# Two load stretches in the middle instead of one, larger output slots, and stores held behind the loads

## The chip, the cores and the metric

The kernel runs on one core of one Trainium2 chip. The metric is the device time of one execution in microseconds (us), the median of three runs. The profiled execution is a further run with its own time.

## The reference

For each of 4096 rows the input `x` has 32 fields of 64 numbers. Every field is multiplied by one 64x64 matrix `W`, and for every pair of fields i < j the output is the elementwise product of field i with the transformed field j:

```python
vid = jnp.einsum('bfd,de->bfe', x, W)
idx_i, idx_j = jnp.triu_indices(32, k=1)
return x[:, idx_i, :] * vid[:, idx_j, :]     # (4096, 496, 64), float32
```

There are 496 pairs, so 33.6 MB are read and 520.1 MB written.

## The kernel before

**Tiles and units.** The host lays the input out so that a partition holds one of 2 x 64 embedding positions and the free dimension holds 128 rows. A *unit* is one field, or one product, of 128 rows: 128 partitions x 128 float32, 512 bytes in a partition and 65,536 bytes in all. A tile is 32 units of input and gives 496 units of output. There are 16 tiles, so 7936 units go out. On-chip memory is one tensor `mem` of 445 units; inputs and finished products share it. The matrix product `vid` of the current tile (32 units) fills all of PSUM.

**Order of the work.** TensorE computes `vid` of a tile in two halves, fields 16 to 31 (high) and then 0 to 15 (low), 8 matmuls each. VectorE (DVE) multiplies pairs, first those among the high fields (120 units), then the 16x16 block of low x high (256 units), then those among the low fields (120 units). When the last product that reads a half of `vid` is done, VectorE raises `free` and TensorE may fill that half for the next tile; it raises `there` when it is full. `by_block` lists the blocks, and `products` cuts them into VectorE instructions where a slot or a seam in it ends (`BREAKS`).

**Slots.** `SLOTS` is a table made ahead by hand or by a planner: entry (size, home, seams...) says that the next `size` units of output are put into `mem` from unit `home` on, and stored with one DMA when they are complete. A seam is a place inside the slot at which an instruction must end, so that the part behind it can wait for something of its own. An instruction that writes units waits until every earlier store that reads those units has landed (`after`).

**Loads.** `GROUPS` says at which tile a group of inputs begins and in which pieces (lowest and highest unit of `mem`) it is loaded. Before, tile 0 comes with two small loads, tiles 1 to 7 with three pieces right behind (224 units), and tiles 8 to 15 with three pieces (256 units) whose DMAs stand in the program at the start of tile 8. A load waits until the units it overwrites have been read and stored.

**The queue.** Every DMA, load or store, is issued by SyncE (SP) in the order of the program (`transfer`, L169). So whatever SP waits for, everything later waits as well. The first store after a group of loads waits for the landing of the last piece but one (`hold[-2]`, L272). `Queue.waits` leaves out waits that an earlier one implies.

Of the kernel before, what the change touches and what calls it, by code (L numbers as in the profile page):

```python
# [10 lines left out]
P = 128  # L11

C = 128
# [1 line left out]
UNITS = 445  # L15


TOP = 256


GROUPS = [
    (0, [(96, 224), (26, 96), (0, 26)]),
    (8, [(154, 256), (26, 154), (0, 26)]),
]


SLOTS = [
# [10 lines left out]
]  # L38


# [4 lines left out]
STARTS = [0, *accumulate(n for n, *_ in SLOTS)]  # L45


BREAKS = sorted({a + s for a, (_, _, *seams) in zip(STARTS, SLOTS) for s in seams} | set(STARTS))


def by_block():


    def within(lo):
        yield "step", lo, 2, 1, 0
        for k in range(2):
            yield "step", lo, 4, 2, k
        for i in (lo, lo + 8):
            yield "row", i + 4, i, 4, 4
        yield "row", lo + 8, lo, 8, 8  # L60

    yield from within(16)
    yield "row", 16, 0, 16, 16
    yield from within(0)


def products(blocks, at=0):

    for kind, a, b, c, d in blocks:
        if kind == "row":  # L70
            rows, n, i0, di, j0, dj = c, d, b, 0, a, 1
        else:
            rows, n, i0, di, j0, dj = 16 // b, c, a, b, a + c + d, b
        r = k = 0
        while r < rows:
            room = BREAKS[bisect_right(BREAKS, at)] - at
            if k or room < n:
                m, w = 1, min(n - k, room)
            else:
                m, w = min(rows - r, room // n), n  # L80
            yield at, m, w, i0 + r * di + k, di, j0 + r * dj, dj
            at += m * w
            if k + w == n:
                r, k = r + m, 0
            else:
                k += w


def pairs(blocks):

    for _, m, w, i, di, j, dj in products(blocks):
        for r in range(m):
            for k in range(w):
                yield i + r * di + k, j + r * dj


class Queue:
# [33 lines left out]
def place_of(t, fields):  # L131

    first = max(begin for begin, _ in GROUPS if begin <= t)
    return TOP - (t - first + 1) * fields


def ends(tiles):
    return [begin for begin, _ in GROUPS[1:]] + [tiles]
# [6 lines left out]
def pairwise_bilinear_kernel(nc, x0, x, out):  # L145
# [5 lines left out]
    HALF = F // 2  # L151

    ctx = ExitStack()
    mem = ctx.enter_context(nc.sbuf_tensor([P, UNITS, C], F32))
    w2 = ctx.enter_context(nc.sbuf_tensor([P, P], F32))
    vid = ctx.enter_context(nc.psum_tensor([P, F, C], F32))

    made = nc.alloc_semaphore("made")
# [3 lines left out]
    behind = {}  # L162
# [4 lines left out]
    def transfer(out_, in_, units, reads, needs):  # L167
        sem = nc.alloc_semaphore(f"moved{len(moved)}")
        sp.issue(lambda: nc.sync.dma_start(out=out_, in_=in_), needs).then_inc(sem, 16)  # L169
        sp.note(sem, 16)  # L170
        moved.append((units, reads, sem))
        return sem

    def after(units):

        needs = [(s, 16) for u, reads, s in moved if reads and overlap(u, units)]
        last = max((n for spans, n in worked if any(overlap(units, s) for s in spans)), default=0)
        return needs + [(made, last)] * (last > 0)

    counts = {made: 0, free: 0}  # L180

    def work(make, spans, needs, tells):


        instruction = dve.issue(make, needs)
        instruction.then_inc(tells, 1)
        counts[tells] += 1
        worked.append((spans, counts[made] + (tells is free)))
        dve.note(tells, counts[tells])

    place = place_of(0, F)
    first = [
        transfer(
            mem[:, :, :].rearrange("p u c -> p (u c)")[:, (place + HALF) * C : (place + F) * C + D],
            x0.rearrange("p u c -> p (u c)")[:, HALF * C : F * C + D],
            (place + HALF, place + F + 1), False, [],
        ),
        transfer(mem[:, place : place + HALF, :], x0[:, :HALF, :], (place, place + HALF), False, []),
    ]
# [8 lines left out]
    owed = 0  # L208
# [3 lines left out]
    def load(g):  # L212
        (begin, pieces), end = GROUPS[g], ends(NT)[g]
        begin = max(begin, 1)
        low = place_of(end - 1, F)
        sems = []
        for lo, hi in pieces:
            at = (begin - 1) * F + lo - low
            sems.append(transfer(mem[:, lo:hi, :], x[:, at : at + hi - lo, :], (lo, hi), False, after((lo, hi))))
            loads.append((range(begin, end), (lo, hi), sems[-1]))  # L220
        return sems

    def loaded(t):
        units = (place_of(t, F), place_of(t, F) + F)
        return [(sem, 16) for tiles, piece, sem in loads if t in tiles and overlap(piece, units)]

    hold = load(0)
    begins = [begin for begin, _ in GROUPS]

    for t in range(NT):  # L230
        if t in begins[1:]:
            hold = load(begins.index(t))
        xs = (place_of(t, F), place_of(t, F) + F)
        xt = mem[:, xs[0] : xs[1], :]
        blocks = list(products(by_block(), t * NP))
        for k, (at, m, w, i, di, j, dj) in enumerate(blocks):
            slot = bisect_right(STARTS, at) - 1
            n = m * w
            begin, end = STARTS[slot], STARTS[slot + 1]
            size, home = SLOTS[slot][:2]  # L240
            units = (home + at - begin, home + at - begin + n)
            ot = mem[:, home : home + size, :]
            o = mem[:, units[0] : units[1], :]
            if m == 1:
                left = xt[:, i : i + w, :]
                right = vid[:, j : j + 1, :].to_broadcast([P, w, C])
            else:
                o = o.rearrange("p (m w) c -> p m w c", m=m)
                right = vid[:, j : j + (m - 1) * dj + 1 : dj, :].unsqueeze(2).to_broadcast([P, m, w, C])
                if di == 0:  # L250
                    left = xt[:, i : i + w, :].unsqueeze(1).to_broadcast([P, m, w, C])
                else:
                    left = xt.rearrange("p (m d) c -> p m d c", d=di)[:, i // di : i // di + m, i % di : i % di + w, :]
            high = j >= HALF
            later = blocks[k + 1 : k + 2]
            owed += not later or high and later[0][5] < HALF
            tells = free if owed and at + n < end else made
            owed -= tells is free
            needs = [(there, 2 * t + 2 - high), *after(units)]
            if tells is free and t + 1 < NT and t + 1 not in begins:  # L260
                needs += loaded(t + 1)
            work(
                lambda: nc.vector.tensor_tensor(o, left, right, ALU.mult),  # L263
                [units, (xs[0] + i, xs[0] + i + w + (m - 1) * di)],
                needs,
                tells,
            )
            at += n
            if at == end:
                needs = [(made, counts[made])]  # L270
                if hold:
                    needs.append((hold[-2], 16))  # L272
                    hold = []
                transfer(out[:, begin:end, :], ot, (home, home + size), True, needs)

    for sem, n in sp.waits([(sem, 16) for _, _, sem in moved]):
        nc.sync.wait_ge(sem, n)
# [60 lines left out]
```

## Time and profile before

| | before |
|---|---|
| median of 3 runs | 1285.02 us (1284.77 to 1285.34) |
| the profiled execution: its time | 1284.47 us |
| the profiled execution: its span | 1283.2 us |
| VectorE busy in the span | 1083.8 us (84%), 341 instructions |
| TensorE busy in the span | 186.5 us (15%), 256 matmuls |
| DMA share, in every one of 40 slices | 90% or more |
| DMA transfers | 83: 8 loads and 75 stores |
| moved | 33.59 MB read, 520.09 MB written |

The span runs from the first to the last instruction of the program. The DMA row of the profile gives the mean busy share of the 16 DMA engines in tenths, slice by slice; the row under it what they moved. Views by windows give the same for chosen stretches. In those a packet counts whole in the window where it starts. With packets of up to 64 KB on 16 engines, about 1 MB may fall on either side of an edge.

### The profile page before, as it was taken

What the parts mean: (1) busy time and instruction counts of PE and PEld (TensorE: products, weight loads), DVE (VectorE), ACT (ScalarE), POOL (GpSimd) and SP (SyncE); (2) the same over time, 40 slices, a digit from 0 to 9 for tenths busy, and PEclk for the clock granted to TensorE, in tenths of its full rate; (3) what the DMA queues carried; (4) which work ended last, traced back from release to release, by engine and by line L of the source; (5) the groups of instructions that cost most, each with busy time, mean ns of one, the idle gap of its engine ahead of it and who ended that gap; (6) DMA issues with size and microseconds to landing.
All of it is one profiled execution on the core that took longest, in us unless ns stands there. A gap on an engine that the chain in (4) does not pass through costs nothing. (4 is left out here: it accounts for less than half of the span.)

```text
span 1283.2 us, 1322 instructions
## 1 busy us (share of the span) xinstructions
PE 186.5 (15%) x256; PEld 72.5 (6%) x256; DVE 1083.8 (84%) x341; POOL 0.2 (0%) x4
## 2 busy tenths in 40 slices
PE   2021120301111030210030111203030110303000
PEld 1000000100000010100010000001010000101000
DVE  6399989989898998998137989988998899999870
POOL 0000000000000000000000000000000000000000
PEclk7556555656555565555565665656555565656555
DMA  9999999999999999999999999999999999999999
GB/s 405 426 433 432 438 433 435 438 435 434 428 433 441 431 436 437 425 433 443 410 421 438 437 433 439 434 429 439 430 436 427 439 427 441 433 436 433 434 422 409
DMA packets 11956, 553.72 MB, mean 432 GB/s; under 512 B 1328, under 2 KB 1328, under 8 KB 1328
## 3 DMA queue, kind: packets, MB, share of 16 engines
q1 hardware_dynamic: 11952, 553.69, 100.0%
q14 instruction: 4, 0.03, 0.0%
HBM read 33.59 MB, written 520.09 MB: 431 GB/s over the span
## 5 line engine op out<-in xcount | busy, mean ns | idle before, releaser
L263 DVE TENSOR_TENSOR mem<-mem,vid 128x1024 f32<-128x1024 f32 (+12 forms) x338 | 1083.3, 3279 | 153.5 <-DMA out_dram<-mem 124.0
L282 PE MATMUL vid<-mem,w 128*128 x256 | 186.5, 897 | 990.3 <-PEq L280 990.3
L282 PEld LDWEIGHTS vid<-mem,w 128*128 128x128 f32 x256 | 72.5, 297 | 1103.5 <-issue 1103.5
L203 DVE COPY w<-mem 64x64 f32<-64x64 f32 x2 | 0.4, 189 | 5.0 <-DMA mem<-in_r_x_dram 4.9
L200 DVE MEMSET w<- 128x128 f32 x1 | 0.2, 165 | 0.8 <-PEq L307 0.8
L307 POOL MEMSET const-bfloat16-1.0<- 128x1 bf16 x1 | 0.1, 101 | 0.0
L307 POOL MEMSET const-uint8-127<- 128x1 uint8 x1 | 0.1, 101 | 0.0
L307 POOL MEMSET const-float32-0.0<- 128x1 f32 x1 | 0.1, 98 | 0.2 <-issue 0.2
L307 POOL MEMSET const-float32-1.0<- 128x1 f32 x1 | 0.1, 98 | 0.0
## 6 DMA issues: line engine op xcount, KB each, us to landing
out_dram<-mem SPq DMA_DIRECT2D x8, 7680.0 KB, 23.4
out_dram<-mem SPq DMA_DIRECT2D x7, 7168.0 KB, 22.8
out_dram<-mem SPq DMA_DIRECT2D x4, 6656.0 KB, 21.8
out_dram<-mem SPq DMA_DIRECT2D x5, 4096.0 KB, 18.8
out_dram<-mem SPq DMA_DIRECT2D x3, 6400.0 KB, 20.0
out_dram<-mem SPq DMA_DIRECT2D x2, 6144.0 KB, 19.9
out_dram<-mem SPq DMA_DIRECT2D x2, 5120.0 KB, 19.3
out_dram<-mem SPq DMA_DIRECT2D x2, 4672.0 KB, 24.4
```

Source lines behind the costliest of these rows:

```text
L200: work(lambda: nc.vector.memset(w2[:, :], 0.0), [], [], made)
L203: lambda: nc.vector.tensor_copy(w2[half, half], mem[half, place + F, :D]),
L263: lambda: nc.vector.tensor_tensor(o, left, right, ALU.mult),
L282: last = nc.tensor.matmul(vid[:, b : b + BANK, :], lhsT=w2[:, :], rhs=xt(b), start=True, stop=True)
L307: nc = _bacc.Bacc("TRN2", target_bir_lowering=False, num_devices=1, dynamic_dma_scratch_size=512)
```

## The change

- `TOP`, `GROUPS`: inputs take 192 units at the most instead of 256. They come as 1 + 5 tiles at the start (160 units behind tile 0, in pieces of 128 and 32), 5 tiles at tile 6 and 5 tiles at tile 11 (160 units each, in pieces of 64, 70 and 26).
- `SLOTS`: 67 slots instead of 75, with other homes and seams. With 10 loads there are 77 transfers instead of 83.
- `STRETCHES`, `store`, `held`: a store of slot 24 or later that is complete before tile 6 begins, or of slot 45 or later before tile 11, is not issued at once but behind the loads of that tile. Slot 24 holds output units 2844 to 2968, all of tile 5 (which ends at 2976); it is the only slot for which this applies, since slot 45 ends in tile 11.
- `by_block`, `products`, `fields`: the triangles of pairs within 16 fields are cut into squares by distance (64, 32, 16 and 8 units), each one nest of up to three loops, instead of pieces of rows and of steps; an instruction may take any whole part of a nest. Where the innermost loop runs along i and j together, both operands are read in runs of several units. 338 products become 247: 128 units x2, 112 x13, 96 x7, 80 x3, 64 x22, 56 x3, 48 x8, 40 x3, 32 x54, 24 x6, 16 x47, 13 x2, 12 x6, 8 x57, 5 x2, 4 x8, 3 x4.

```diff
-TOP = 256
+TOP = 192
 GROUPS = [
-    (0, [(96, 224), (26, 96), (0, 26)]),
-    (8, [(154, 256), (26, 154), (0, 26)]),
+    (0, [(32, 160), (0, 32)]),
+    (6, [(128, 192), (58, 128), (32, 58)]),
+    (11, [(128, 192), (58, 128), (32, 58)]),
 ]
+STRETCHES = [24, 45]
 SLOTS = [
-    (116, 256), (73, 372), (59, 240, 16), (60, 299), (73, 372), (67, 240), (72, 307), (64, 379), (96, 240, 67),
-    (108, 336, 43), (112, 208, 32), (100, 320, 16), (64, 192), (92, 256, 64), (97, 348), (119, 192, 64),
...
+    (120, 192), (128, 312), (128, 176, 16), (108, 312), (76, 176), (88, 252), (96, 340), (112, 176, 76),
+    (128, 288, 52), (128, 144, 32), (128, 272, 16), (128, 112, 32), (128, 240, 32), (88, 96, 16), (120, 184, 56),
+    (128, 304), (128, 80), (128, 208), (128, 64), (128, 192, 16), (120, 320), (128, 48), (124, 192), (128, 316),
+    (124, 192), (128, 316), (128, 176, 16), (120, 304, 12), (88, 176), (104, 264), (72, 368), (128, 176, 88),
+    (128, 304, 64), (128, 144, 32), (128, 272, 32), (128, 112, 32), (128, 240, 32), (104, 112), (104, 216, 24),
+    (120, 320), (128, 80), (128, 208), (124, 64, 16), (127, 188, 20), (128, 315), (125, 192), (128, 317),
+    (128, 176, 16), (120, 304, 13), (88, 176), (88, 264, 40), (88, 352), (128, 176, 88), (128, 304, 48),
+    (128, 144), (128, 272, 32), (96, 112, 32), (112, 208, 64), (112, 320), (128, 112), (128, 240, 80),
+    (128, 80, 32), (120, 208, 32), (117, 328), (123, 64), (128, 187), (128, 315),
 ]
 def by_block():
-    def within(lo):
-        yield "step", lo, 2, 1, 0
-        for k in range(2):
-            yield "step", lo, 4, 2, k
-        for i in (lo, lo + 8):
-            yield "row", i + 4, i, 4, 4
-        yield "row", lo + 8, lo, 8, 8
-    yield from within(16)
-    yield "row", 16, 0, 16, 16
-    yield from within(0)
+    def within(lo, fields):
+        n, many = fields // 2, 1
+        while n:
+            yield ((many, fields // many, 0), (n, 0, 1), (n, 1, 1)), lo, lo + fields - 2 * n + 1
+            n, many = n // 2, many * 2
+    yield from within(16, 16)
+    yield ((1, 0, 0), (16, 0, 1), (16, 1, 0)), 0, 16
+    yield from within(0, 16)
...
+    held = []
+    def store(slot, last):
+        nonlocal hold
+        begin, end = STARTS[slot : slot + 2]
+        home = SLOTS[slot][1]
+        units = (home, home + end - begin)
+        needs = [(made, last)]
+        if hold:
+            needs.append((hold[-2], 16))
+            hold = []
+        transfer(out[:, begin:end, :], mem[:, units[0] : units[1], :], units, True, needs)
     for t in range(NT):
         if t in begins[1:]:
             hold = load(begins.index(t))
+            for late in held:
+                store(*late)
+            held = []
...
             if at == end:
-                needs = [(made, counts[made])]
-                if hold:
-                    needs.append((hold[-2], 16))
-                    hold = []
-                transfer(out[:, begin:end, :], ot, (home, home + size), True, needs)
+                late = (slot, counts[made])
+                group = sum(behind <= slot for behind in STRETCHES)
+                if t < begins[group]:
+                    held.append(late)
+                else:
+                    store(*late)
```

More of the change, by code (lines that the diff above doesn't have):

```diff
@@ L51, in by_block @@
 def by_block():
-    def within(lo):
-        yield "step", lo, 2, 1, 0
-        for k in range(2):
-            yield "step", lo, 4, 2, k
-        for i in (lo, lo + 8):
-            yield "row", i + 4, i, 4, 4
-        yield "row", lo + 8, lo, 8, 8
-    yield from within(16)
-    yield "row", 16, 0, 16, 16
-    yield from within(0)
-def products(blocks, at=0):
[L69 to L86, printed above, removed]
@@ L89, in pairs @@
-def pairs(blocks):
[L91 to L94, printed above, removed]
+    def within(lo, fields):
[6 more added lines that the diff above has]
+    yield from within(0, 16)
@@ new lines, in products @@
+def products(blocks, at=0):
+    for nest, i, j in blocks:
+        units = [n for n in accumulate((n for n, _, _ in nest[:0:-1]), lambda a, b: a * b, initial=1)][::-1]
+        r, size = 0, units[0] * nest[0][0]
+        while r < size:
+            room = min(BREAKS[bisect_right(BREAKS, at)] - at, size - r)
+            level = next(k for k, unit in enumerate(units) if r % unit == 0 and room >= unit)
+            count = nest[level][0]
+            part = min(count - r // units[level] % count, room // units[level])
+            places = [r // unit % n for unit, (n, _, _) in zip(units, nest)]
+            yield (
+                at,
+                part * units[level],
+                ((part, *nest[level][1:]), *nest[level + 1 :]),
+                i + sum(k * di for k, (_, di, _) in zip(places, nest)),
+                j + sum(k * dj for k, (_, _, dj) in zip(places, nest)),
+            )
+            at += part * units[level]
+            r += part * units[level]
@@ new lines, in pairs, with steps, fields @@
+def pairs(blocks):
+    def steps(nest, i, j):
+        if not nest:
+            yield i, j
+            return
+        (n, di, dj), *inner = nest
+        for k in range(n):
+            yield from steps(inner, i + k * di, j + k * dj)
+    for _, _, nest, i, j in products(blocks):
+        yield from steps(nest, i, j)
+def fields(a, lo, steps, whole):
+    first = a[:, lo : lo + 1, :]
+    dims = [[step * C, n] for n, step in steps if n > 1 or whole]
+    dims = [*dims[:-1], [1, dims[-1][1] * C]] if whole else [*dims, [1, C]]
+    return bass.AP(first.tensor, first.offset, [list(first.ap[0]), *dims])
@@ L232, in pairwise_bilinear_kernel @@
             hold = load(begins.index(t))
+            for late in held:
+                store(*late)
+            held = []
         xs = (place_of(t, F), place_of(t, F) + F)
-        xt = mem[:, xs[0] : xs[1], :]
         blocks = list(products(by_block(), t * NP))
-        for k, (at, m, w, i, di, j, dj) in enumerate(blocks):
+        for k, (at, n, nest, i, j) in enumerate(blocks):
             slot = bisect_right(STARTS, at) - 1
-            n = m * w
             begin, end = STARTS[slot], STARTS[slot + 1]
-            size, home = SLOTS[slot][:2]
+            home = SLOTS[slot][1]
             units = (home + at - begin, home + at - begin + n)
[L242 to L253, printed above, removed]
+            whole = nest[-1][1:] == (1, 1)
+            inner = [n for n in accumulate((c for c, _, _ in nest[:0:-1]), lambda a, b: a * b, initial=1)][::-1]
+            o = fields(mem, units[0], [(c, step) for (c, _, _), step in zip(nest, inner)], whole)
+            left = fields(mem, xs[0] + i, [(c, step) for c, step, _ in nest], whole)
+            right = fields(vid, j, [(c, step) for c, _, step in nest], whole)
+            top = i + sum((c - 1) * step for c, step, _ in nest)
             high = j >= HALF
             later = blocks[k + 1 : k + 2]
-            owed += not later or high and later[0][5] < HALF
+            owed += not later or high and later[0][4] < HALF
             tells = free if owed and at + n < end else made
@@ L263, in pairwise_bilinear_kernel @@
                 lambda: nc.vector.tensor_tensor(o, left, right, ALU.mult),
-                [units, (xs[0] + i, xs[0] + i + w + (m - 1) * di)],
+                [units, (xs[0] + i, xs[0] + top + 1)],
                 needs,
```

8 rows, old and new, of the table SLOTS are left out of this document.

## The prediction

> **What bounds the kernel now.** I read the page from the top: the busy shares, the slices and then the costliest group.
>
> ```profile
> span 1283.2 us, 1322 instructions
> PE 186.5 (15%) x256; PEld 72.5 (6%) x256; DVE 1083.8 (84%) x341; POOL 0.2 (0%) x4
> ...
> DMA  9999999999999999999999999999999999999999
> GB/s 405 426 433 432 438 433 435 438 435 434 428 433 441 431 436 437 425 433 443 410 421 438 437 433 439 434 429 439 430 436 427 439 427 441 433 436 433 434 422 409
> DMA packets 11956, 553.72 MB, mean 432 GB/s; under 512 B 1328, under 2 KB 1328, under 8 KB 1328
> ...
> L263 DVE TENSOR_TENSOR mem<-mem,vid 128x1024 f32<-128x1024 f32 (+12 forms) x338 | 1083.3, 3279 | 153.5 <-DMA out_dram<-mem 124.0
> ```
>
> VectorE is idle for 153.5 us, 124.0 of them until a store has landed. The DMA engines have no slice below nine tenths. So VectorE waits for the DMA queue and not the other way round. Next I ask windows for the rate, away from the ends and around the loads at tile 8.
>
> ```profile
> core 0: us, PE busy (x) PEld busy (x) DVE busy (x) POOL busy (x), PEclk, DMA share, GB/s
> 60.00:560.00 500.00, 84.95 (x112) 32.83 (x112) 465.12 (x156) 0.00 (x0) 0.56 1.00 434
> 560.00:760.00 200.00, 20.55 (x32) 8.11 (x32) 135.96 (x52) 0.00 (x0) 0.55 1.00 431
> 760.00:1260.00 500.00, 71.47 (x96) 27.67 (x96) 454.01 (x120) 0.00 (x0) 0.56 1.00 434
> 2.30:60.00 57.70, 9.57 (x16) 3.90 (x16) 28.58 (x14) 0.00 (x0) 0.64 1.00 428
> 0.00:2.29 2.29, 0.00 (x0) 0.00 (x0) 0.17 (x1) 0.20 (x4) 1.00 0.43 63
> ```
>
> The share is 1.00 throughout, and the rate without loads is 434 GB/s. 553.72 MB at 434 take 1275.9 us. The span is 7.3 us more: about 2.3 before the first packets; 0.8 in the first loads (57.7 us at 428); 1.4 in the loads of tile 8 (200 us at 431); the rest lies in the ramp after the last packets and in the rounding of the rate (half a GB/s is 1.5 us). The change can reach only the terms that depend on transfers and loads, unless the queue runs dry. A measurement here can tell about 0.2%, or 2.6 us, from no change.
>
> **The change, part by part.** The bytes don't change: 480 units of loads (224 + 256 before, 3 x 160 after) and 7936 units of stores. At 434 GB/s a unit of 65,536 bytes takes 0.151 us.
>
> *Six transfers fewer* (83 to 77). A fixed price of a transfer would show where stores are small:
>
> ```profile
> 690.00:850.00 160.00, 21.73 (x32) 8.51 (x32) 151.27 (x57) 0.00 (x0) 0.57 1.01 435
> 950.00:1110.00 160.00, 29.29 (x38) 11.50 (x39) 149.42 (x43) 0.00 (x0) 0.57 1.00 433
> ...
> L169 SPq DMA_DIRECT2D out_dram<-mem x13: 332/332/333, 700.0 to 848.1; - x13
> ...
> L169 SPq DMA_DIRECT2D out_dram<-mem x9: 332/332/333, 963.2 to 1103.1; - x9
> ```
>
> 13 issues in the one stretch and 9 in the other, and the one with more is 2 GB/s faster, 0.7 us. The edges of a window are uncertain by 1 MB, 2.4 us, so four transfers cost 1.7 us at most: between 0 and 0.4 each. I exclude less than nothing, as another transfer brings no bytes forward. I take 0.1, near the row's sign: -0.5 us, with ends 0 and -2.4. The Trainium skill, in "DMA: Bandwidth & Descriptors", section on the anatomy of one DMA (SWDGE path), gives a DMA a fixed 2.0 us beside its bytes, which would make this -12 us as an estimate; the trace, with 83 transfers back to back, has no room for that, since 166 us are not there.
>
> *A second stretch of loads.* The slices with the loads of tile 8 are the 410 and 421 above. 200 us at 431 instead of 434 lose 1.4 us; a narrower window gives more:
>
> ```profile
> 590.00:720.00 130.00, 10.11 (x16) 4.04 (x16) 69.03 (x32) 0.00 (x0) 0.53 1.00 426
> ```
>
> 130 us at 426 lose 2.4. Two stretches of 160 units replace one of 256. If the loss goes with the bytes, the second costs a quarter of 1.4, +0.35; if with the turn from writing to reading and back, all of it. I take +1.4, the wider window with the smaller error of its edges, and as ends +0.35 and +2.4. A gain is excluded, as both windows and both slices are below the others.
>
> *Products: 338 to 247, in other forms.* Times by form:
>
> ```profile
> L263 DVE TENSOR_TENSOR mem<-mem,vid 128x8192 f32<-128x8192 f32 x25 | 216.9, 8681 | 4.2 <-DMA out_dram<-mem 4.2
> L263 DVE TENSOR_TENSOR mem<-mem,vid 128x2048 f32<-128x2048 f32 x81 | 181.9, 2281 | 9.7 <-DMA out_dram<-mem 9.7
> L263 DVE TENSOR_TENSOR mem<-mem,vid 128x1024 f32<-128x1024 f32 x118 | 137.7, 1215 | 52.9 <-PE vid L282 29.2 <-DMA out_dram<-mem 23.5
> L263 DVE TENSOR_TENSOR mem<-mem,vid 128x4096 f32<-128x4096 f32 x15 | 66.1, 4416 | 19.4 <-DMA out_dram<-mem 19.4
> L263 DVE TENSOR_TENSOR mem<-mem,vid 128x14336 f32<-128x14336 f32 x3 | 45.2, 15080 | 0.0
> ```
>
> 64 units less 8 units are 7.466 us: 0.133 us a unit, and 0.15 for the instruction. 338 x 0.15 + 7936 x 0.133 would be 1108.8 us. The group is busy for 1083.3, so neighbours overlap and an instruction costs about 0.075. 91 fewer save some 7 us of VectorE. They are worth nothing, since the 153.5 idle us of VectorE hide them. That the new nests have the same price a unit is not shown by the trace; see the second rival.
>
> *Does the queue stay full?* At four kinds of place it could run dry. The latencies come from the first load:
>
> ```profile
> 0.73 2.54 SPq L169 DMA_DIRECT2D mem<-in_r_x_dram  x5
> 13.15 28.20 DVE L263 TENSOR_TENSOR mem<-mem,vid 128x1024 f32<-128x1024 f32 x12 [6.81 <-PE vid L282]
> ...
> mem<-in_r_x_dram SPq DMA_DIRECT2D x2, 1664.0 KB, 28.0
> mem<-in_r_x_dram SPq DMA_DIRECT2D x1, 1056.0 KB, 5.1
> ...
> 654.34 6.70 PE vid L282 x8
> ```
>
> 63 GB/s until 2.29 are 0.14 MB, or one 8.4 KB packet on each engine: from the issue at 0.73 all 16 have begun in 1.6 us. The 1056 KB need 2.5 us and land 5.1 after the issue, so a landing is reported about 1.0 after the last byte.
>
> (a) The first store. Its 120 units are four products of 64, 32, 16 and 8, together 16.6 us from 13.15: ready at 29.7, on all engines by 31.3. The loads ahead of it (1056 + 1024 KB and 160 units, 12.6 MB) end at 2.3 + 29.5 = 31.8 at 428 GB/s. Margin 0.5 us; without it the gap is what is missing, below 1 us.
>
> (b) The held store. SP comes to slot 24 after the three loads of tile 6 and waits there for the second to land. Queued behind it on SP are only later stores. The last piece, 26 units (1664 KB), takes 3.9 us; less 1.0 and 1.6, margin 1.3. This is the order that the loads of tile 8 have now, with a last piece of the same size, and the share stayed 1.00. Slot 25 needs tile 6: its first piece (64 units, 9.7 us), 1.0 to land, 6.7 for a half on TensorE, 16.6 for 120 units, 34.0 us from the start of the loads. Loads and store 24 keep the queue busy for 284 units, 42.9 us. At tile 11 no store is held; the order of waits is the same.
>
> (c) Slot 26, and 47 alike. Its last 112 units lie where store 24 is read from. So 1.0 + 15.1 us after store 24 it is ready, and 1.6 later sending; store 25 (128 units) lasts 19.3. Margin 1.6.
>
> (d) Runs in which the slots grow. Slot 4 (from unit 176) waits for store 2 (from 176) to land. Then VectorE makes 76 units in 10.4 us while store 3 (108 units, 16.3 us) goes out: a lead of 16.3 - 1.0 - 10.4 = 4.9 us. Slots 5 to 8 have 424 units, 57.4 us with a dozen instructions; stores 4 to 7 have 372, 56.2. At slot 8 the lead is 3.7; less 1.6, margin 2.1. After the stretches the same happens at slots 31 and 52: 392 units in four slots against 384 in four stores, 58.0 - 1.0 - 53.5 = 3.5, margin 1.9.
>
> All margins are positive, so I book nothing for gaps. The sum against the profiled execution's own 1284.47 (span 1283.2, 1.3 around it): 1284.47 - 0.5 + 1.4 = 1285.4. The median of the runs shown is 0.55 above that execution, so the forecast is **1285.9 us**, from 1285.02: no change that can be told.
>
> **Rivals.**
>
> *Faster: transfers do have a price.* If each costs the bound of 0.4, six save 2.4; if besides the load loss goes with bytes (+0.35) and the first loads, now 160 units instead of 224, lose 0.6 instead of 0.8, the time is 1285.02 - 2.4 + 0.35 - 0.2 = 1282.8, still just inside 0.2%. Only with 0.5 or more a transfer is it outside, 1282.2. Against it speaks that the stretch with more stores was the faster one. The skill's 2.0 us belongs here too; by it alone the estimate would be 1273, less than the bytes and the start need.
>
> *Slower: the new nests are dearer on VectorE and the queue runs dry behind growing slots.* In the triangles (240 of 496 units) both operands now step in overlapping runs; no row shows that form. The place is slot 8, and slots 31 and 52. It decides from where 67.8 us of VectorE (slots 4 to 8) grow by 2.1, 3%, or 6% if the triangles alone grow. At 7% slot 8 comes 2.6 late and slots 31 and 52 each 3.7 - 1.9 = 1.8, together 6.2: 1292.1. For it: VectorE is 84% busy and not far from the bound. Against it: five forms with different reads all lie on one line of 0.133 a unit.
>
> *Slower: the second stretch costs more than the first.* At 2.4 or more for the second, and with (a) and (b) missing their margins by half a microsecond in each of three places, 1285.02 + 2.4 - 0.5 + 1.5 = 1288.4. For it: margins (a) and (b) are the thinnest. Against: the same hand-over left no hole at tile 8.
>
> *The change does less than it says:* only one store is held, and none at tile 11. Then its order matters little and the time is the forecast's.
>
> **How the numbers follow.** The forecast with its last rival 0.80; faster 0.06; dearer nests 0.07; a dear second stretch 0.07. By the bounds of the two booked terms the likeliest case runs from 1285.02 + 0.35 - 2.4 = 1283.0 to 1285.02 + 2.4 = 1287.4, its ends unlikely. I give 1284.0 to 1288.4: it leaves out the dearer nests, the faster rival and the lowest end. Faster 0.06, same 0.80, slower 0.14.
>
> **What would show it.** Right: DMA share at 1.00 in all windows, 434 GB/s away from loads, two dips of 1 to 2.5 us instead of one, VectorE idle for more than 153 us and nearly all behind stores, 112 units still near 15.1 us. Wrong: a slice of DMA below nine tenths near 31, 160, 485, 600 or 1000 us; a triangle of 64 units over 8.9 us; or a store-only window off 434.

## The result, and the profile after

| | before | after |
|---|---|---|
| median of 22 runs each | 1284.86 us (1284.34 to 1285.49) | 1286.76 us (1284.92 to 1288.20) |
| ratio, 95% interval | | 1.0015 (1.0009 to 1.0021) |
| profiled execution, time and span | 1284.47, 1283.2 us | 1286.34, 1285.0 us |

The changed kernel is 1.9 us slower, 0.15%: inside the 0.2% that the prediction called no change, but clear of noise by the interval. Forecast were 1285.9 and +0.9 us. The runs of the changed kernel also spread over 3.3 us, those of the kernel before over 1.2. The page after, with the rows that answer to those of before:

```profile
span 1285.0 us, 1230 instructions
PE 179.1 (14%) x256; PEld 70.1 (5%) x256; DVE 1078.4 (84%) x250; POOL 0.2 (0%) x4
...
DMA  9999999999999999999999999999999999999999
GB/s 423 420 428 443 424 455 426 424 439 443 424 424 441 439 409 434 430 440 435 432 439 435 424 441 432 439 408 412 423 441 435 428 447 426 441 432 441 424 439 394
DMA packets 11091, 553.71 MB, mean 431 GB/s; under 512 B 1232, under 2 KB 1232, under 8 KB 1232
...
L285 DVE TENSOR_TENSOR mem<-mem,vid 128x4096 f32<-128x4096 f32 (+12 forms) x247 | 1077.8, 4430 | 167.2 <-DMA out_dram<-mem 122.8
```

The bytes are the same, the DMA row has no slice under nine tenths, and VectorE still waits for stores. The one dip of before (410, 421) has become two: 409 in slice 15, and 408, 412, 423 in slices 27 to 29. The second is deeper and longer. Windows around both, columns as before:

```profile
core 0: us, PE busy (x) PEld busy (x) DVE busy (x) POOL busy (x), PEclk, DMA share, GB/s
2.30:60.00 57.70, 9.54 (x16) 3.90 (x16) 45.37 (x9) 0.00 (x0) 0.64 1.03 444
60.00:430.00 370.00, 59.42 (x80) 23.13 (x80) 339.75 (x74) 0.00 (x0) 0.57 1.00 432
430.00:530.00 100.00, 9.56 (x16) 3.87 (x16) 57.44 (x16) 0.00 (x0) 0.53 1.01 433
530.00:840.00 310.00, 46.19 (x64) 17.93 (x64) 282.90 (x71) 0.00 (x0) 0.57 1.00 434
840.00:930.00 90.00, 9.60 (x16) 3.90 (x16) 53.77 (x15) 0.00 (x0) 0.54 1.00 419
930.00:1230.00 300.00, 44.79 (x64) 17.39 (x64) 277.70 (x62) 0.00 (x0) 0.56 1.00 433
```

The window around tile 6 has 433 GB/s, which its edges don't let us tell from the 434 without loads. That around tile 11 runs at 419: 90 us x 15/434 = 3.1 us lost, more than the 2.4 us that the edges can make. The two stretches load the same number of units in the same pieces, so turns between writing and reading alone should not make them differ. The timeline around tile 11 shows what does (start, duration, engine, what; in brackets the idle time before and who ended it):

```profile
846.15 16.01 DVE L285 TENSOR_TENSOR mem<-mem,vid 128x640 f32<-128x640 f32 x5 [6.08 <-DMA out_dram<-mem]
883.31 8.75 DVE L285 TENSOR_TENSOR mem<-mem,vid 128x1024 f32<-128x1024 f32 x2 [21.15 <-PE vid L305]
877.11 9.60 PE L305 MATMUL vid<-mem,w 128*128 x16 [86.15 <-PEq L303]
846.19 38.70 SPq L183 DMA_DIRECT2D mem<-in_r_x_dram  x3
884.56 0.33 SPq L183 DMA_DIRECT2D mem<-in_r_x_dram  x1
```

SP begins the three loads at 846.19, but issues the third only at 884.56, 1.25 us after the first product of tile 11 began. VectorE had ended tile 10 at 862.16. The chain of waits has TensorE's first half of tile 11:

```profile
877.11 6.18 PE vid L305 x8
```

**Theory A, the late third load.** The third piece overwrites units 32 to 58, the input of tile 10. It waits for the last product of that tile. That product raised `free` for TensorE, not `made`, and a product noted so is waited for by the next count of `made` (`counts[made] + (tells is free)`). The next `made` is the first product of tile 11. It needs the first piece landed (1.0 us) and a half on TensorE (6.2); the third load is issued 1.25 later and needs up to 1.6 to send on all engines. That is 10.1 us from the end of the first piece, and what TensorE takes to start after a landing. The second piece, 70 units, covers 10.6. It is a tie. At tile 6 the same piece lies on the input of tile 4, long read. **Theory B:** a stretch costs 1.5 to 2.5 us through its turns, whatever its pieces.

### The profile page after: what moved, and what is told of

Same layout as the page of the kernel before. It is cut to its first block, busy times and chain, and to the rows that moved or that the text cites. A ratio compares the mean times of both kernels' runs of the same rounds, so it can differ in the third digit from the quotient of the medians.

```text
span 1285.0 us, 1230 instructions
## 1 busy us (share of the span) xinstructions
PE 179.1 (14%) x256; PEld 70.1 (5%) x256; DVE 1078.4 (84%) x250; POOL 0.2 (0%) x4
## 5 line engine op out<-in xcount | busy, mean ns | idle before, releaser
L285 DVE TENSOR_TENSOR mem<-mem,vid 128x4096 f32<-128x4096 f32 (+12 forms) x247 | 1077.8, 4430 | 167.2 <-DMA out_dram<-mem 122.8
L305 PE MATMUL vid<-mem,w 128*128 x256 | 179.1, 866 | 1019.2 <-PEq L303 1019.2
```

Source lines behind the costliest of these rows:

```text
L305: last = nc.tensor.matmul(vid[:, b : b + BANK, :], lhsT=w2[:, :], rhs=xt(b), start=True, stop=True)
```

## Experiments

All times are medians. The kernel before stood at 1284.75 (experiments 1, 2, 4, 5), 1284.76 (experiment 3 and three of the runs of 6) and 1284.43 us (the others) beside the three sets of runs; the changed kernel's 1286.76 is from the runs of the result.

**1. A first piece that lands earlier.**

```diff
-    (11, [(128, 192), (58, 128), (32, 58)]),
+    (11, [(160, 192), (58, 160), (32, 58)]),
```

> At tile 11 the 160 units of loads come in pieces of 32, 102 and 26 units instead of 64, 70 and 26; nothing else differs. Theory A: the third load waits for the first product of tile 11, which waits for the landing of the first piece and one half on TensorE, and it reaches SP about 1 us too late to follow the second piece, so the queue runs dry at 885 us and the third load's packets start cold. Then a first piece that lands 5 us earlier takes that away: 1.5 to 1.9 us faster than the changed kernel, 1285.0 to 1285.3 us, and the runs spread less. Theory B: a second stretch of loads costs 1.5 to 2.5 us by its turns between writing and reading: no change, 1286.8 us.

Measured: 1284.80 us (1284.44 to 1285.21, 11 runs), 2.0 faster than the changed kernel, and a spread of 0.8 us instead of 3.3.

```profile
846.46 32.86 SPq L183 DMA_DIRECT2D mem<-in_r_x_dram  x3
877.74 13.08 DVE L285 TENSOR_TENSOR mem<-mem,vid 128x1024 f32<-128x1024 f32 x3 [15.31 <-PE vid L305]
878.99 0.33 SPq L183 DMA_DIRECT2D mem<-in_r_x_dram  x1
```

```profile
840.00:930.00 90.00, 9.19 (x16) 3.75 (x16) 54.17 (x16) 0.00 (x0) 0.56 1.00 427
```

The third load goes out at 878.99, again 1.25 us after the first product began, 5.6 earlier than in the changed kernel, and the window has 427 GB/s instead of 419 (1.7 us, inside the error of the edges; it is the medians that decide). Theory A.

**2. A second piece that ends earlier.**

```diff
-    (11, [(128, 192), (58, 128), (32, 58)]),
+    (11, [(128, 192), (84, 128), (32, 84)]),
```

> At tile 11 the pieces are 64, 44 and 52 units instead of 64, 70 and 26: the second ends 3.9 us earlier, while the third is issued at the same time. Theory A (the late third load): the queue stays dry for 3.5 to 4 us longer, 1290.3 to 1290.8 us. Theory B (the turns): 1286.8 us.

Measured: 1289.49 us (1289.12 to 1291.61, 5 runs), 2.7 more than the changed kernel; the profiled executions, 1290.68 and 1286.34, differ by 4.3. That is 0.8 less than A asked for in the median, and far from B's nothing.

```profile
884.62 0.33 SPq L183 DMA_DIRECT2D mem<-in_r_x_dram  x1
```

```profile
880.00:887.00 7.00, 6.76 (x13) 2.48 (x12) 3.63 (x2) 0.00 (x0) 0.84 0.41 132
840.00:930.00 90.00, 9.73 (x16) 3.90 (x16) 50.88 (x14) 0.00 (x0) 0.54 0.95 396
```

The third load is issued at the same time as in the changed kernel, while the second ends earlier. From 880 to 887 us the queue is 0.41 busy, and the 90 us run at 396 GB/s, 4.8 us below the 419 of the changed kernel.

**3. The wait itself taken away, the pieces kept.** The slot ends with tile 10, so its last product raises `made`. Being complete before tile 11, the slot of 117 units also becomes a held store, which stands ready behind the loads.

```diff
-    (125, 192), (128, 317),
+    (117, 192), (8, 309), (128, 317),
```

> Slot 45 is cut in two, 117 units that end with tile 10 and 8 units of tile 11; loads and their pieces are those of the changed kernel. The last product of tile 10 then raises made itself, as it completes a slot, and the third load need not wait for the first product of tile 11. Theory A (the late third load): it is issued near 861 us instead of 885, the hole at 885 us is gone, 1.5 to 2 us faster than the changed kernel: 1284.8 to 1285.3 us. Theory C (the pieces themselves matter, since a first piece of 32 units healed it): 1286.8 us.

Measured: 1284.71 us (1284.56 to 1285.10, 11 runs).

```profile
846.34 16.32 SPq L183 DMA_DIRECT2D mem<-in_r_x_dram  x3
```

```profile
840.00:930.00 90.00, 12.00 (x16) 4.61 (x16) 54.37 (x16) 0.00 (x0) 0.56 1.00 429
```

All three loads are out by 862.66, with TensorE and the first product as late as ever (877.34 and 882.76). The held store doesn't explain the gain: it waits for the second piece and goes out at 887.27, and the store in its place went out at 887.01 in the changed kernel. So it is the wait and not the pieces: theory A in its details, and C falls.

The packets of the traces, each with a start, a duration and a size, show what the late load costs. In the changed kernel only 6 of the 16 DMA engines are busy at 885.25 us; that gap is 0.5 us of all engines. Behind it the 128 packets of the third load take 0.68 us each instead of 0.50 here, another 1.4 us. Together 1.9. In experiments 1 and 3 no engine runs dry there.

Both remedies together:

> The slot cut at the end of tile 10 and the pieces of 32, 102 and 26 units together. If each alone has already taken away the whole hole: 1284.7 us, as each alone, and so level with the kernel before. If something of it was left: a few tenths less.

Measured: 1284.78 us (11 runs). Nothing was left to heal. The changed kernel with either remedy is level with the kernel before; no version was found that beats it.

**4. The held store.**

```diff
-STRETCHES = [24, 45]
+STRETCHES = []
```

> Undoes one part of the change: no store is held, so the store of slot 24 stands in the queue ahead of the loads of tile 6. If the held store is what keeps the DMA queue full over that stretch: VectorE has slot 24 ready near 460 us, it goes out for 18.7 us, the loads begin near 481 instead of 462 us, the first piece lands near 492, TensorE needs 7 us and VectorE 16 us more, so slot 25 can go out near 517 us; the loads end near 505 us. A hole of 11 to 12 us, time 1298 us. If the order of that one store does not matter, as one of my rivals had it: 1286.8 us, like the changed kernel.

Measured: 1297.22 us (1296.57 to 1298.05, 4 runs), 10.5 more.

```profile
DMA  9999999999999996999999999999999999999999
GB/s 418 437 428 429 441 421 449 423 439 437 421 449 427 427 411 293 421 441 433 421 453 421 437 423 451 412 452 417 419 439 438 444 425 424 434 437 449 423 437 392
```

A window, and the timeline's row of VectorE:

```profile
500.00:520.00 20.00, 3.70 (x9) 1.33 (x7) 19.66 (x6) 0.00 (x0) 0.66 0.45 191
```

```profile
500.30 35.33 DVE L285 TENSOR_TENSOR mem<-mem,vid 128x8192 f32<-128x8192 f32 x7 [36.67 <-PE vid L305]
```

VectorE waits 36.67 us for tile 6 and begins at 500.30; from 500 to 520 us the queue is 0.45 busy, 11 us empty. One held store is worth over 10 us: it is the cover while tile 6 comes in.

**5. The products cut as before**, with everything else changed (the functions `by_block` and `products` of the kernel before).

> Undoes another part: the products are cut as in the kernel before (rows and steps), with the changed kernel's slots, loads and held store. About 90 more products at 0.075 us each, 7 us of VectorE. If VectorE's time is covered, as I forecast: 1286.8 us, at most 0.5 more, from the first store, whose margin was 0.5 us. If the margins at the growing slots are used up by it: 1 to 3 us more and holes near 160, 600 and 1005 us.

Measured: 1286.44 us (1285.67 to 1287.27, 11 runs), inside the spread of the changed kernel.

```profile
L279 DVE TENSOR_TENSOR mem<-mem,vid 128x1024 f32<-128x1024 f32 (+10 forms) x307 | 1081.6, 3596 | 164.0 <-DMA out_dram<-mem 119.3 <-PE vid L299 44.6
```

There are 307 products, 60 more than 247 (with larger slots fewer cuts fall than in the 338), for 3.8 us more of VectorE, 0.063 each. The idle time hides them.

**6. The queue alone.** A kernel of DMAs without products: 62 stores of 128 units from one block and 16 loads of one tile, and only the place of the loads changes. (`LOADS` lists: before which store, from which tile, to which.)

```diff
 LOADS = [(0, 0, 8), (31, 8, 16)]                        # one stretch
+LOADS = [(0, 0, 6), (23, 6, 11), (42, 11, 16)]          # two
+LOADS = [(0, 0, 1), (4, 1, 2), (8, 2, 3), ...           # fifteen of one tile
+LOADS = [(0, 0, 4), (5, 4, 5), (10, 5, 6), ...          # twelve of one tile
```

> No products and no TensorE: the queue alone. 62 stores of 128 units of one constant block, and 16 loads of one tile each, 8 at the start and 8 in one stretch in the middle; never fewer than two transfers queued. The output is a constant. This gives the level for the next two: near 1282 us by the bytes at 434 GB/s, a start of 2.3 us and an end of 1.

> The queue alone, with the same 78 transfers, but the loads as 6 at the start and two stretches of 5. The output is a constant. If the price of a stretch lies in its two turns: 1.1 to 1.4 us more than with one stretch. If it lies in the bytes loaded between stores: 0.3 us more at the most.

> The queue alone, with the same 78 transfers, but 1 load at the start and 15 stretches of a single tile. The output is a constant. If the price lies in the turns: 14 times 1.1 to 1.4, 15 to 20 us more than with one stretch. If in the bytes: as with one stretch, within 1 us.

> The queue alone, with 78 transfers, 4 loads at the start and 12 stretches of a single tile. The run with 15 singles had a hole of 11 us at its start, where the first store waited for its block, and this one loads enough ahead. The output is a constant. If the price lies in the turns: 11 stretches more than with one, at 0.8 to 1.7 each 9 to 18 us above 1284.5. If in the bytes: within 1 us of it.

Measured: 1284.47, 1286.14, 1306.71 and 1300.19 us. The first is 2.5 above the 1282 expected, and the second stretch costs 1.7, more than the 1.1 to 1.4 expected. The run with fifteen was spoilt at its start, where its first slice has 257 GB/s instead of 398: 32.7 us x 141/434 = 10.6 us of hole, the wait for the block to store. Without it 14 stretches cost 11.6, 0.8 each; eleven more in the run with twelve cost 15.7, 1.4 each. That the price goes with the bytes alone is excluded; between 0.8 and 1.7 us of the whole time remain for a stretch. The pages of one and of twelve stretches:

```profile
GB/s 398 436 435 429 427 447 431 427 443 433 431 427 447 431 427 443 433 431 425 428 419 451 429 429 431 445 427 431 447 429 429 427 449 427 431 447 429 429 427 394
```

```profile
DMA  9999999999999999999999999999999999999995
GB/s 391 442 426 444 426 446 417 435 438 421 444 426 446 422 424 444 424 444 426 432 434 424 442 426 446 416 435 436 419 443 426 441 424 432 426 430 444 426 430 232
```

With twelve the last slice is only half busy (232 GB/s). A window of the last 20 us, again of one and of twelve stretches:

```profile
1280.00:1300.00 20.00, 0.00 (x0) 0.00 (x0) 1.00 0.01 3
1280.00:1300.00 20.00, 0.00 (x0) 0.00 (x0) 1.00 0.21 92
```

The profiled executions of the two differ by 16.4 us. Counted by packets (the next section says how), only 5.1 of them are lost in the stretches, about 0.5 each; 11.3 lie behind 1278 us, where the 16 engines run out one after the other, the last at 1299. So most of this price is not a slower queue: with the turns the engines end apart, and the last one sets the time. For the second stretch (1.7) the shares are 0.7 and 0.9.

> The queue alone, loads as 6 + 5 + 5, but each store of 128 units is two of 64, 140 transfers instead of 78. The output is a constant. If a transfer costs only its descriptors, about 0.08 us by the packets of the traces: 5 us more than with 62 stores, 1291 us. By the upper bound of my prediction, 0.4 each: 25 us more. By the fixed 2.0 us that the Trainium skill gives in DMA: Bandwidth & Descriptors: 124 us more, an estimate.

Measured: 1290.65 us (1290.57 to 1290.81, 4 runs), 4.5 more than with 62 stores, 0.073 for each of 62 further transfers. The packets bear this out: between 60 and 400 us, with stores alone, one of 64 KB takes 2.418 us and two of 32 KB take 2.426 (medians). A transfer has 128 packets, 8 on each engine, which makes 0.06 us.

## Why the prediction was right, and which step was not

Windows have edges that are uncertain by 2.4 us. The packets allow a finer count: each is credited to a stretch by the part of its time that lies in it, and what a stretch moves less than 434 GB/s is its loss. In us, from one profiled execution of each kernel:

| loss | before | changed | experiment 1 | experiment 3 | both |
|---|---|---|---|---|---|
| first loads, 5 to 60 us | 0.7 | 0.1 | 0.1 | 0.6 | 0.1 |
| loads of tile 8 (610 to 700) or 6 (440 to 530) | 1.5 | 1.4 | 1.2 | 1.0 | 1.4 |
| loads of tile 11, 840 to 910 | | 3.3 | 1.2 | 1.3 | 1.5 |
| the rest up to 1278, stores alone | 1.3 | 0.3 | 0.9 | 0.5 | 0.4 |
| behind 1278 | 0.8 | 1.1 | 1.6 | 1.2 | 1.1 |
| time of the execution | 1284.47 | 1286.34 | 1285.01 | 1284.70 | 1284.55 |

- **The bound** held: 432, 434 and 433 GB/s in the long windows between the loads (the first within its edges of 434), and VectorE idle for 167.2 us, 122.8 behind stores (before 153.5 and 124.0). "Nearly all behind stores" was not so: 44.2 us are waits for TensorE, at the two stretches and at the start.
- **Six transfers fewer, -0.5:** right in size, as far as the queue alone shows it. 6 x 0.073 is -0.44, inside the bounds 0 and -2.4, and by the table above the stores alone lose 0.5 to 1.0 less than before. The faster rival needed 0.5 a transfer and falls. By the fixed 2.0 us that the Trainium skill gives in "DMA: Bandwidth & Descriptors", section on the anatomy of one DMA, the 62 further transfers would have cost 124 us, as an estimate, if nothing hid it. They cost 4.5, so in a full queue it is hidden.
- **A second stretch, +1.4:** right. The 1.4 and the 0.8 that were read from windows of before are 1.5 and 0.7 by packets. With the late load healed, the two stretches together lose 2.3 to 2.9 us against the one of before with 1.5: the second costs 0.8 to 1.4. Yet the healed kernel is level with before (+0.05, -0.05 and +0.35 us by experiments 1, 3 and both), and not 0.9 above; each interval alone reaches 0.1%, 1.2 us, to either side, and it is that the three agree that speaks for it. The table shows what the sum left out: the first loads lose 0.1 to 0.7 us less, the stores alone 0.5 to 1.0 less where 0.5 was booked, and the end loses 0.4 to 0.8 more. Why the first loads lose less, and lose 0.1 us in one execution and 0.6 in another though nothing in them differs, stays open.
- **The products:** 91 fewer cost VectorE 5.5 us less (1083.3 to 1077.8; I had 7), worth nothing, as forecast. The dearer nests fall by the trace:

```profile
L285 DVE TENSOR_TENSOR mem<-mem,vid 128x4096 f32<-128x4096 f32 x54 | 237.9, 4413 | 12.1 <-DMA out_dram<-mem 12.1
L285 DVE TENSOR_TENSOR mem<-mem,vid 128x14336 f32<-128x14336 f32 x13 | 196.1, 15082 | 30.7 <-DMA out_dram<-mem 30.7
L285 DVE TENSOR_TENSOR mem<-mem,vid 128x8192 f32<-128x8192 f32 x22 | 190.9, 8681 | 33.5 <-PE vid L305 23.1 <-DMA out_dram<-mem 10.5
```

  4413, 15082 and 8681 ns against 4416, 15080 and 8681.
- **The places where the queue could run dry:** (a), (c) and (d) held; no slice or window shows a hole at 31, 160, 524, 600 or 1005 us. So did (b) at tile 6; and that holding one store matters little is refuted by 10.5 us.
- **The step that failed** is the last sentence of (b): "At tile 11 no store is held; the order of waits is the same." I asked when slot 25 and store 24 would be ready, and took for granted that the loads themselves go out together. They do at tile 6 (all three within 3.87 us from 431.24 on), not at tile 11. The trace of before had it, for tile 8:

```profile
617.71 44.93 SPq L169 DMA_DIRECT2D mem<-in_r_x_dram  x3
661.06 16.61 DVE L263 TENSOR_TENSOR mem<-mem,vid 128x1024 f32<-128x1024 f32 x8 [22.39 <-PE vid L282]
662.31 0.33 SPq L169 DMA_DIRECT2D mem<-in_r_x_dram  x1
```

  Three loads over 44.93 us, the third 1.25 us after the first product of tile 8: the same wait. It cost nothing then, because the second piece had 128 units, 19.3 us. The change put 70 units there, 10.6 us, against a chain of 10 to 11. This is worth 2.0 us (1286.76 against 1284.80 and 1284.71) and makes the spread.

So the two booked terms hold, and a 2.0 us wait was missing from the sum. That the total still lies within 1 us of the forecast is partly luck: gains that were not booked, 0.2 to 1.0 us net by the executions of the table, stand against the missing wait, and the allowance of 0.55 for the median against the profiled execution came to 0.4 in both kernels.

## What to carry to other kernels

Where the DMA queue is the bound, list for every issue after the first in a stretch what its engine waits for, loads included, and set that chain against what is still queued at that time. A wait that costs nothing before may be paid as soon as the transfer ahead of it gets shorter. A wait counted on a shared semaphore can stand for a later instruction than the one that is meant; ending a unit of work where the data is last read takes that away.

## What the runs showed of the hardware

In a busy queue a stretch of loads between stores lost 1.0 to 1.6 us in the packets for five and eight tiles, and 0.5 on average for one tile, against 0.06 to 0.07 us for a further transfer. The time of the whole run can rise by more, since the 16 engines end apart: I had expected the price of a transfer to be small, but not that the order of the same transfers could cost 15.7 us, most of it at the end. A queue that ran partly dry for less than 2 us lost 0.5 us in the gap and 1.4 us more in slower packets behind it. Why the engines end apart, and why the packets behind a gap are slower, stays open.
